# Turning softmax's exponentials by plain products with the identity instead of TensorE's transpose mode

## The chip, the cores and the metric

The kernel runs on one core of one Trainium2 chip. The metric is device time in microseconds (us), median of three runs. The core has TensorE (PE in the profile; its weight loads are PEld), VectorE (DVE), ScalarE (ACT), GpSimd (POOL) and SyncE (SP), each of which works through its own instructions in order and waits on the others by semaphores. Every one of the program's times below is of the whole kernel unless a stretch is named.

## The reference

Eight images of 384 channels and 32 x 32 = 1,024 positions go through two layers, all in fp32. Cut to what matters:

```python
# layer 0: a Mamba block, forward and backward over the 1,024 positions, and a 3x3 depthwise convolution
deltaA  = exp(delta[..., None] * A)                     # 384 channels x 16 states
deltaBu = (delta * u)[..., None] * Bm
h = dA * h + dBu                                        # the scan, step by step
y = einsum('bdn,bn->bd', h, c)                          # summed over the 16 states
...
# layer 1: causal attention with 6 heads of 64, then a feed-forward net with binarized weights
qkv    = x @ Wqkv
scores = einsum('bhqd,bhkd->bhqk', q, k)                # 1,024 x 1,024 for each head
scores = where(causal, scores, -inf)
attn   = softmax(scores, axis=-1)
out    = einsum('bhqk,bhkd->bhqd', attn, v)
out    = out @ Wproj + bproj
...
t = t + attention(layernorm(t)); t = t + feed_forward(layernorm(t))
```

The feed-forward part gives values for five of the eight images (its groups leave the others zero), so the kernel computes it for five.

## The kernel before

The kernel runs the scan of one image beside the attention and feed-forward of the one before it. The steps of both are emitted interleaved, and a scheduler puts each engine's instructions in order. The last image's attention has no scan left to run beside it.

Matrix results go into eight PSUM banks, shared by name; `s` and `pt` have two each:

```python
BANKS = {"y": 1, "da": 2, "s": 2, "pt": 2, "av": 1}
QT = 4              # blocks of 128 queries in a half of 512
...
ptp = ctx.enter_context(tc.tile_pool(name="ptp", bufs=2))
```

The scan works on units of two states. GpSimd multiplies twice for each unit, VectorE scans, and TensorE sums the states into `y`, each block transposed on the way, with the transpose mode. The buffer `g` (7 of them) is free again when that sum has read it.

```python
def s_first(u):
    g = sp.tile([P, 2, HB], F32, name=f"g_{u.name}", tag="g", bufs=7)
    ...
    pin(nc.gpsimd.tensor_tensor(g, ud, sst.pop(("bc", 0, u.name)), ALU.mult))          # L564
...
def s_scan(u):
    ...
        nc.scalar.activation(da, sst["dl", u.b, u.c, u.part], AF.Exp, scale=...)       # L577
        ...
        nc.vector.tensor_tensor_scan(gi[:, ::step], da[:, ::step], gi[:, ::step], ...) # L582
    ...
    pin(nc.gpsimd.tensor_tensor(g, g, sst.pop(("bc", 1, u.name)), ALU.mult))           # L588
...
def s_sum(u):
    ...
    for i in range(2):
        for j in range(QT):
            nc.tensor.matmul(                                                          # L598
                out=y[:, j, :], lhsT=g[:, i, chunk(j)], rhs=ident, is_transpose=True,
                start=(opens and i == 0 and j == 0), stop=(closes and i == 1),
                skip_group_check=True,
            )
```

The attention works on two heads at a time (`e`), over 512 queries (`g`). Scores come with queries on the partitions; the exponentials `pr` leave ScalarE together with their row sums:

```python
def scores(i, qi, n, kb, k0, k1):
    ...
    ss = [bank(f"s_{b}_{c}_{qi}_{kb}_{e}", "s") for e in range(2)]
    for e in range(2):
        nc.tensor.matmul(out=ss[e][:, : k1 - k0], lhsT=st["q"][rows_of(e), c, chunk(qi)],
                         rhs=st["k"][rows_of(e), c, k0:k1], start=True, stop=(k1 < n)) # L753
    ...
    for e in range(2):
        ...
        nc.vector.tensor_reduce(m, s, AX.X, ALU.max, negate=True)                      # L773
        nc.scalar.activation(pr, s, AF.Exp, bias=m, accum_out=rs[:, i, e, kb : kb + 1])# L774
```

To weigh the values, the keys must lie on the partitions. So each 128 x 128 block of `pr` is turned by TensorE into a `pt` bank, ScalarE copies the bank to `ptn`, and the product with `v` sums into `av`. The factors that normalize are spread over the partitions by plain products with the identity:

```python
def spread(kb):
    ...
    nc.tensor.matmul(out=fp[rows_of(e), chunk(i)], lhsT=f.to_broadcast([P, HD]),
                     rhs=ident, start=True, stop=True)                                 # L811
...
def turned(j):
    cols = slice(max(j - g * QT, 0) * P, HB)
    for e in range(2):
        pt = bank(f"pt_{b}_{c}_{g}_{j}_{e}", "pt")
        for i in range(max(j - g * QT, 0), QT):
            nc.tensor.transpose(                                                       # L825
                pt[:, chunk(i)], st["pr", c, g, i, e][:, chunk(j)], ident
            )
        ptn = ptp.tile([P, HB], F32, name=f"ptn_{b}_{c}_{g}_{j}_{e}", tag=f"ptn{e}")
        nc.scalar.copy(ptn[:, cols], pt[:, cols])                                      # L829
        st["ptn", j, e] = ptn

def weigh(j):
    ...
        nc.tensor.matmul(out=av[rows_of(e), cols],
                         lhsT=st["v"][:, j, hd * HD : (hd + 1) * HD],
                         rhs=st["ptn", j, e][:, cols],
                         start=(j % QT == 0), stop=(j % QT == QT - 1))                 # L839
```

For each image and pair of heads, the first 512 queries need 10 turned blocks for a head and the second 512 need 26, as blocks above the diagonal are left out: 36 x 6 heads x 8 images = 1,728 blocks, in 576 banks.

Of the kernel before, what the change touches and what calls it, by code (L numbers as in the profile page):

```python
# [52 lines left out]
def kernel(  # L53
# [16 lines left out]
    nc = tc.nc  # L70
# [11 lines left out]
    def ctile(name, shape, dt=F32):  # L82
        return const.tile(shape, dt, name=name, tag=name)
# [4 lines left out]
    def mtile(name, n=L):  # L88
        return mid.tile([P, n], F32, name=name, tag="mid")
# [7 lines left out]
    def bank(name, tag=None):  # L97
        if tag is None:
            turn[0] += 1
            tag = ("s", "pt")[turn[0] % 2]  # L100
        return ps.tile([P, HB], F32, name=name, tag=tag, bufs=BANKS[tag])

    def half(h):
        return slice(h * HB, (h + 1) * HB)

    def chunk(c):
        return slice(c * P, (c + 1) * P)
# [29 lines left out]
    for d in range(2):  # L137
        nc.scalar.dma_start(out=wdt[d * DW : d * DW + RANK, :], in_=w_dt)
        nc.scalar.dma_start(
            out=wdt[d * DW + RANK : d * DW + RANK + 1, :],  # L140
# [13 lines left out]
    ident = ctile("ident", [P, P])  # L154
# [491 lines left out]
    def attention(b, emit_ffn, emit):  # L646
        st = {}
# [82 lines left out]
        def rows_of(e):  # L730
            return slice(e * HD, (e + 1) * HD)
# [52 lines left out]
        def weighted_values(c, g, steps):  # L784


            last = (g + 1) * QT - 1

            def factors():

                nm, rs = st["nm", c, g], st["rs", c, g]
                st["f", c, g] = mtile(f"f_{b}_{c}_{g}").rearrange("p (k l) -> p k l", k=2)
                if g == 0:
                    nc.vector.reciprocal(rs, rs)
                    return
                low = small.tile([P, QT, 2, 1], F32, name=f"low_{b}_{c}", tag="low")
                nc.vector.tensor_reduce(low, nm, AX.X, ALU.min)
                nc.vector.tensor_tensor(nm, low.to_broadcast([P, QT, 2, 2]), nm, ALU.subtract)
                nc.scalar.activation(nm, nm, AF.Exp)
                nc.vector.tensor_tensor(rs, rs, nm, ALU.mult)  # L800
                nc.vector.tensor_reduce(low, rs, AX.X, ALU.add)
                nc.vector.reciprocal(low, low)
                nc.vector.tensor_tensor(rs, nm, low.to_broadcast([P, QT, 2, 2]), ALU.mult)

            def spread(kb):

                fp = bank(f"f_{b}_{c}_{g}_{kb}")
                for i in range(QT):
                    for e in range(2):
                        f = st["rs", c, g][:, i, e, kb : kb + 1]  # L810
                        nc.tensor.matmul(  # L811
                            out=fp[rows_of(e), chunk(i)],
                            lhsT=f.to_broadcast([P, HD]),
                            rhs=ident,
                            start=True,
                            stop=True,
                        )
                nc.scalar.copy(st["f", c, g][:, kb, :], fp)

            def turned(j):  # L820
                cols = slice(max(j - g * QT, 0) * P, HB)
                for e in range(2):
                    pt = bank(f"pt_{b}_{c}_{g}_{j}_{e}", "pt")
                    for i in range(max(j - g * QT, 0), QT):
                        nc.tensor.transpose(  # L825
                            pt[:, chunk(i)], st["pr", c, g, i, e][:, chunk(j)], ident
                        )
                    ptn = ptp.tile([P, HB], F32, name=f"ptn_{b}_{c}_{g}_{j}_{e}", tag=f"ptn{e}")
                    nc.scalar.copy(ptn[:, cols], pt[:, cols])  # L829
                    st["ptn", j, e] = ptn  # L830

            def weigh(j):
                if j % QT == 0:
                    st["av"] = bank(f"av_{b}_{c}_{g}_{j}", "av")
                av = st["av"]
                cols = slice(max(j - g * QT, 0) * P, HB)
                for e in range(2):
                    hd = 2 * c + e
                    nc.tensor.matmul(  # L839
                        out=av[rows_of(e), cols],  # L840
                        lhsT=st["v"][:, j, hd * HD : (hd + 1) * HD],
                        rhs=st["ptn", j, e][:, cols],
                        start=(j % QT == 0),
                        stop=(j % QT == QT - 1),
                    )
                if j % QT < QT - 1:
                    return
                kb = j // QT
                o, f = st["o"][:, c, half(g)], st["f", c, g][:, kb, :]
                if kb == 0:  # L850
                    nc.vector.tensor_tensor(o, av, f, ALU.mult)  # L851
                else:
                    nc.vector.tensor_tensor(av, av, f, ALU.mult)
                    nc.vector.tensor_tensor(o, o, av, ALU.add)

            for j in range(last + 1):

                @steps
                def _(j=j):
                    if j == 0:  # L860
                        factors()
                    if j % QT == 2:
                        spread(j // QT)
                    turned(j)
                    if j > 0:
                        weigh(j - 1)

            @steps
            def _():
                weigh(last)  # L870
# [302 lines left out]
```

## Time and profile before

| | |
|---|---|
| time, median of 3 runs | 5232.83 us (5232.45 to 5233.16) |
| span of the profiled execution | 5243.0 us |
| granted TensorE clock, mean | 0.864 |
| VectorE busy | 3565.3 us, 68% |
| ScalarE busy | 2726.2 us, 52% |
| turning products (L825): TensorE busy | 312.3 us, 1,728 instructions |
| copies of turned blocks (L829): ScalarE busy | 259.4 us, 576 instructions |
| DMA: moved | 1199.86 MB, mean 229 GB/s |

A line of the profile names a source line of the kernel, an engine, an operation, and what is written and read. "Busy" merges overlapping instructions. TensorE's products overlap one another, and the ends of their records are modelled, so their durations hold a latency; the distance from one start to the next is what a product takes of the engine. In the 40 slices of the page, a digit is a share in tenths of a slice of 131 us. The granted clock is the share of full TensorE clock that was allowed. A wait is idle time of an engine together with the instruction that ended it.

### The profile page before, as it was taken

The numbers are of one execution on the slowest core, as the hardware profiler recorded it, in microseconds if no ns is written. First come the engines' busy times: TensorE is split into PE (matmuls) and PEld (weight loads), VectorE is DVE, ScalarE is ACT, GpSimd is POOL, SyncE is SP. The second block draws the span as 40 slices with busy tenths as digits, with TensorE's granted clock in tenths as the row PEclk, the third lists the DMA queues.
The fourth block names the chain that finished last, engine by engine and source line by source line (L and its number), as shares of the span: only waits on it lengthen the run. The fifth ranks groups of instructions, "written<-read, shape, count | busy, mean of one in ns | idle before, by whom it ended". The sixth has DMA issues, their size and how long they took to land.

```text
span 5243.0 us, 52624 instructions
## 1 busy us (share of the span) xinstructions
PE 4173.2 (80%) x16458; PEld 2200.6 (42%) x16458; DVE 3565.3 (68%) x4249; ACT 2726.2 (52%) x4914; POOL 3674.0 (70%) x1932
## 2 busy tenths in 40 slices
PE   5466566889778889777897788888888888888899
PEld 1223333444334444334443444444444544444444
DVE  6998887667786668766677766677666666566422
ACT  4665554455644555645556445565355354464434
POOL 0477675977768786769876697767787977887700
PEclk7667576989888899889898789998888999999989
DMA  6768678757678567686676875666866866667500
GB/s 227 277 239 283 228 266 284 242 191 263 225 249 292 196 231 240 214 299 227 232 248 223 276 251 201 230 229 231 301 221 211 277 215 239 210 207 236 189 29 25
DMA packets 625121, 1199.86 MB, mean 229 GB/s; under 512 B 44440, under 2 KB 103240, under 8 KB 624840
## 3 DMA queue, kind: packets, MB, share of 16 engines
q1 hardware_dynamic: 615328, 1180.34, 65.6%
q10 hardware_dynamic: 9512, 16.15, 0.9%
q8 instruction: 130, 2.13, 0.2%
q14 instruction: 151, 1.24, 0.1%
HBM read 1030.65 MB, written 165.68 MB: 228 GB/s over the span
## 4 chain that ended last, share of the span: by engine, by line
POOL 32%; issue 20%; PE 13%; DVE 12%; DMA 8%; ACT 4%; SPq 1%; POOLq 0%; DVEq 0%; ACTq 0%
POOL g L564 18%; POOL g L588 13%; DMA bc<-rows 6%; DVE g L582 5%; PE s L753 2%; PE y L598 1%; PE yp L1000 1%; PE qp L697 1%; PE av L839 1%; DVE dp L515 1%; DVE u L362 1%; DVE loc L383 1%; PE hp L955 1%; PE pt L825 1%; PE op L667 1%
## 5 line engine op out<-in xcount | busy, mean ns | idle before, releaser
L564 POOL TENSOR_TENSOR g<-ud,bc 128x1024 f32<-128x1024 f32 x768 | 1830.0, 2383 | 832.9 <-PE y L598 410.4
L588 POOL TENSOR_TENSOR g<-g,bc 128x1024 f32<-128x1024 f32 x768 | 1819.9, 2370 | 311.6 <-issue 135.6
L577 ACT ACTIVATE da<-dl,amat 128x512 f32<-128x512 f32 x1536 | 1057.9, 692 | 1622.5 <-DVE g L582 1577.5
L582 DVE TENSOR_TENSOR_SCAN g<-da,g 128x512 f32<-128x512 f32 x768 | 905.7, 1210 | 551.9 <-POOL g L564 518.2
L598 PE MATMUL y<-ident,g 128*128 128x128 f32 x6144 | 963.2, 304 | 368.3 <-POOL g L588 344.7
L582 DVE TENSOR_TENSOR_SCAN g<-da,carry,g 128x512 f32<-128x512 f32 x768 | 955.4, 1271 | 420.0 <-POOL g L564 399.2
L598 PEld LDWEIGHTS y<-ident,g 128*128 128x128 f32 x6144 | 792.3, 157 | 801.5 <-POOL g L588 480.7
L753 PE MATMUL s<-k,q 64*128 64x512 f32 (+3 forms) x1152 | 464.4, 601 | 177.6 <-ACT pr L774 140.1
L773 DVE TENSOR_REDUCE nm<-s 128x1 f32<-128x512 f32 (+3 forms) x576 | 300.6, 545 | 268.5 <-PE s L762 200.0
L774 ACT ACTIVATE pr<-s,nm 128x512 f32<-128x512 f32 (+3 forms) x576 | 329.5, 575 | 157.5 <-DVE nm L773 150.5
L839 PE MATMUL av<-ptn,v 128*64 128x512 f32 (+3 forms) x1152 | 367.8, 544 | 27.7 <-DVE o L851 22.0
L955 PE MATMUL hp<-t,w 128*128 128x512 f32 x720 | 336.7, 612 | 34.8 <-DMA w<-w1s 20.6
L336 PE MATMUL in<-xn,win 128*128 128x512 f32 x576 | 299.6, 665 | 69.7 <-ACT up L343 36.9
L825 PE MATMUL pt<-ident,pr 128*128 128x128 f32 x1728 | 312.3, 305 | 38.6 <-ACT ptn L829 29.9
L1000 PE MATMUL yp<-h,w 128*128 128x512 f32 x720 | 327.9, 614 | 2.5 <-DMA w<-w2s 2.5
L829 ACT COPY ptn<-pt 128x512 f32<-128x512 f32 (+3 forms) x576 | 259.4, 480 | 125.4 <-PE pt L825 123.6
L753 PEld LDWEIGHTS s<-k,q 64*128 64x128 f32 x1152 | 162.7, 205 | 338.3 <-ACT pr L774 216.9
L825 PEld LDWEIGHTS pt<-ident,pr 128*128 128x128 f32 x1728 | 212.9, 154 | 171.3 <-ACT ptn L829 79.9
L697 PE MATMUL qp<-t,wqk 128*128 128x512 f32 x576 | 265.8, 609 | 13.3 <-DVE t L300 13.3
L383 DVE SCALAR_TENSOR_TENSOR loc<-xn,vec,loc 128x496 f32<-128x496 f32 (+3 forms) x384 | 257.2, 721 | 4.1 <-ACT loc L373 4.0
L362 DVE SCALAR_TENSOR_TENSOR u<-up,vec,u 128x512 f32<-128x512 f32 (+3 forms) x288 | 201.1, 744 | 27.8 <-ACT u L352 27.5
L1000 PEld LDWEIGHTS yp<-h,w 128*128 128x128 f32 x720 | 140.2, 198 | 176.9 <-issue 176.9
(154 smaller groups left out, 4536.6 us busy)
## 6 DMA issues: line engine op xcount, KB each, us to landing
bc<-rows SPq DMA_DIRECT2D x1536, 512.0 KB, 4.9
t<-st SPq DMA_DIRECT2D x63, 512.0 KB, 6.0
su<-u SPq DMA_DIRECT2D x48, 512.0 KB, 4.2
du<-su SPq DMA_DIRECT2D x96, 256.0 KB, 4.7
sdl<-du SPq DMA_DIRECT2D x96, 256.0 KB, 2.9
sud<-du SPq DMA_DIRECT2D x96, 256.0 KB, 3.2
ud<-sud SPq DMA_DIRECT2D x96, 256.0 KB, 5.2
dl<-sdl SPq DMA_DIRECT2D x96, 256.0 KB, 5.6
```

The source lines that it names most:

```text
L564: pin(nc.gpsimd.tensor_tensor(g, ud, sst.pop(("bc", 0, u.name)), ALU.mult))
L577: nc.scalar.activation(da, sst["dl", u.b, u.c, u.part], AF.Exp, scale=amat[:, u.c, n : n + 1])
L582: nc.vector.tensor_tensor_scan(gi[:, ::step], da[:, ::step], gi[:, ::step], first, ALU.mult, ALU.add)
L588: pin(nc.gpsimd.tensor_tensor(g, g, sst.pop(("bc", 1, u.name)), ALU.mult))
L598: nc.tensor.matmul(out=y[:, j, :], lhsT=g[:, i, chunk(j)], rhs=ident, is_transpose=True, start=(opens and i == 0 and j == 0), stop=(closes ...
L697: nc.tensor.matmul(out=qp, lhsT=st["wqk"][:, c, o : o + P], rhs=st["xn"][:, c, half(h)], start=(c == 0), stop=(c == NC - 1),)
L753: nc.tensor.matmul(out=ss[e][:, : k1 - k0], lhsT=st["q"][rows_of(e), c, chunk(qi)], rhs=st["k"][rows_of(e), c, k0:k1], start=True, stop=(k ...
L774: nc.scalar.activation(pr, s, AF.Exp, bias=m, accum_out=rs[:, i, e, kb : kb + 1])
L825: nc.tensor.transpose(pt[:, chunk(i)], st["pr", c, g, i, e][:, chunk(j)], ident)
L839: nc.tensor.matmul(out=av[rows_of(e), cols], lhsT=st["v"][:, j, hd * HD : (hd + 1) * HD], rhs=st["ptn", j, e][:, cols], start=(j % QT == 0 ...
L955: nc.tensor.matmul(out=hp, lhsT=st["w1"][:, c, chunk(m % 2)], rhs=st["xn"][:, c, half(h)], start=(c == 0), stop=(c == NC - 1),)
L1000: nc.tensor.matmul(out=yp, lhsT=st["w2", k // 6][:, k % 6, :], rhs=st["h", k // NC][:, k % NC, half(h)], start=(k == 0), stop=(k == NF - 1),)
```

## The change

The products that turn `pr` lose the transpose mode. The same block is the stationary operand and the same identity the moving one, but the array multiplies and adds in fp32, as in every plain product of this kernel[...]. The result is the same block, turned. Nothing else is edited; the sums of `y`, which use the transpose mode too, stay as they are. The change asks whether the mode is worth having for these blocks.

```diff
--- before.py
+++ after.py
@@ -822,8 +822,12 @@
                 for e in range(2):
                     pt = bank(f"pt_{b}_{c}_{g}_{j}_{e}", "pt")
                     for i in range(max(j - g * QT, 0), QT):
-                        nc.tensor.transpose(
-                            pt[:, chunk(i)], st["pr", c, g, i, e][:, chunk(j)], ident
+                        nc.tensor.matmul(
+                            out=pt[:, chunk(i)],
+                            lhsT=st["pr", c, g, i, e][:, chunk(j)],
+                            rhs=ident,
+                            start=True,
+                            stop=True,
                         )
                     ptn = ptp.tile([P, HB], F32, name=f"ptn_{b}_{c}_{g}_{j}_{e}", tag=f"ptn{e}")
                     nc.scalar.copy(ptn[:, cols], pt[:, cols])
```

The scheduler sees a product of another kind, and so the order of instructions on TensorE, VectorE, ScalarE and the DMA queue differs between the two programs from the first turned blocks on; GpSimd's order is the same.

## Prediction

> **What bounds the kernel now.** I read the page first, for the shape of the whole; then a table of busy time over the stretches in which the softmax runs; then who waits for whom in one of them; last the durations and spacing of TensorE's instructions, for prices. From the page, the busy totals and three rows of its 40 slices (131 us each):
>
> ```profile
> PE 4173.2 (80%) x16458; PEld 2200.6 (42%) x16458; DVE 3565.3 (68%) x4249; ACT 2726.2 (52%) x4914; POOL 3674.0 (70%) x1932
> ...
> PE   5466566889778889777897788888888888888899
> ...
> POOL 0477675977768786769876697767787977887700
> PEclk7667576989888899889898789998888999999989
> ```
>
> From slice 7 on, TensorE (PE) and GpSimd (POOL) are both nearly full; the last two slices belong to TensorE alone. No engine is full throughout, so what counts is what happens where the change is. The turning products (line 825) lie in eight stretches, 216 in each, one per image. The table of busy time by stretch (width, PE, PE weight loads, DVE, ACT, POOL, granted clock, DMA share, GB/s), first and last stretch and the sum of all eight:
>
> ```profile
> 995.00:1218.00 223.00, 186.91 (x988) 100.36 (x986) 144.63 (x179) 128.77 (x300) 181.50 (x94) 0.92 0.62 213
> ...
> 5063.00:5221.00 158.00, 149.46 (x672) 65.58 (x672) 47.58 (x101) 79.58 (x222) 0.00 (x0) 0.89 0.03 11
> sum 1724.00, PE 1463.82 PEld 782.01 DVE 1040.40 ACT 976.07 POOL 1245.19; mean PE 182.98 PEld 97.75 DVE 130.05 ACT 122.01 POOL 155.65
> ```
>
> The last stretch has no scan beside it and TensorE is idle for 158 - 149.5 = 8.5 us of it: TensorE-bound. In the other seven (1,566 us together) PE is busy 1,314 us and idle 252, POOL busy 1,245 and idle 321. Both are 80 to 84% full, and the totals don't say which leads. The waits do. Waits of PE and then of POOL in the stretch 995 to 1218 (us in total, times, longest):
>
> ```profile
> PE s L753 <- ACT pr L774: 17.7, 15, 4.5
> PE f L811 <- DVE rs L803: 5.3, 2, 3.5
> ...
> POOL g L564 <- PE y L598: 36.7, 17, 8.5
> POOL g L564 <- PE s L762: 3.4, 1, 3.4
> ```
>
> POOL is idle 41.5 us there, and 36.7 of it waits for TensorE's y products to free a g buffer. TensorE never waits for POOL there: its own gaps are the softmax's chain (a score bank not yet read by ScalarE). The same two lines lead in the other stretches I opened (46.3 and 46.7 us of POOL's waits at 3114 to 3339 and 4176 to 4409). So in these stretches TensorE, working in order, sets the pace, and POOL follows.
>
> **Prices from the trace.** Durations by line (min/median/max ns): the turning products, and two plain fp32 products for comparison, factors (64 stationary columns) and scores (128):
>
> ```profile
> L825 PEld LDWEIGHTS pt<-ident,pr x1728: 137/141/231, 994.8 to 5221.1; 128*128 128x128 f32 x192
> L825 PE MATMUL pt<-ident,pr x1728: 272/273/477, 994.9 to 5221.2; 128*128 128x128 f32 x192
> ...
> L811 PEld LDWEIGHTS f<-ident,rs x1152: 132/137/232, 1020.1 to 5219.3; 128*64 128x64 f32 x192
> ...
> L753 PEld LDWEIGHTS s<-k,q x1152: 182/186/335, 982.2 to 5199.5; 64*128 64x128 f32 x192
> ```
>
> The code has 1,728 turns, and they are 1,728 instructions. It has 576 factor products, and they are 1,152: a plain fp32 product is two instructions, each with its own weight load. The timeline gives the spacing:
>
> ```profile
> 1999.59 2.56 PE L598 MATMUL y<-ident,g 128*128 128x128 f32 x22
> ...
> 4048.60 5.15 PE ap L896 x12
> ...
> 4601.83 0.55 PE L825 MATMUL pt<-ident,pr 128*128 128x128 f32 x3 [0.91 <-ACT ptn L829]
> ...
> 5132.27 0.49 PE L753 MATMUL s<-k,q 64*128 64x128 f32 x4
> ```
>
> A duration holds a latency that overlaps, so I take spacing. 22 transposes in the y sums: (2.56 - 0.27) / 21 = 109 ns each. Plain: 12 passes of 512 columns in 5.15 us (a piece of the chain) = 429 ns each, so 128 columns take 107 ns a pass. Hence a turn goes from one pass of 109 to two of about 109.
>
> A first product after idleness also shows its weight load. Three transposes took 0.55 us: 0.55 - 0.27 - 0.11 = 0.17 to the second one, 56 over 109. The scores (two heads side by side, two passes) took 0.49: 0.22 to the second pass, some 105 over. So a group that starts cold of weights pays 50 ns more.
>
> **What the Trainium skill says.** "TensorE: Matmul & The Clock Gate", Terms, calls the transpose mode four times faster for FP32. Here both the passes (one against two) and the weight load's visible part (56 against 105 ns) say two. "Perfetto Trace Analysis", Transposes: use transpose rather than a standard matmul; the direction agrees. The first page's Part 4 says that the 8/8 clock doesn't engage for transposes; the trace disagrees, as the 22 above ran at 109 ns, the speed of plain passes. So I count no clock gained merely because the turns become plain. Its LDWEIGHTS section gives columns / 1.2 ns, an estimate of 107 for 128; this agrees with 186 - 137 = 49 ns between 128 and 64 columns and with the 105 above. A plain load thus still fits behind a pass of 109.
>
> **The change in parts.**
> 1. More passes: 1,728 x 109 ns = 188 us at full clock. The stretches have a granted clock near 0.90: 188 / 0.90 = 209 us.
> 2. Weight loads in sight: the turns come in 576 groups (1 to 4 each). I choose half of them as starting bare: 288 x 50 ns = 14 us. In all 223 us of TensorE, 28 for each image.
> 3. Last image: PE is idle 8.5 us of 158, so nearly all counts: 26 us.
> 4. Other seven images: 7 x 28 = 196 us. TensorE is the pace there, but it idles 36 us a stretch, half of that waiting for ScalarE to free a score bank. Work put between two such waits shortens the second; against that, a turned group is delivered up to 0.5 us later (4 x 109 + 50 ns), and the copies to ptn stand in ScalarE's order beside the exponentials. And a fuller TensorE holds its clock longer: 0.90 to 0.93 would give back 3% of 1,314 us, 40 us. I choose half of the 196 as hidden or given back: 98 remain.
> 5. Nothing is moved by hand, but the scheduler orders the program anew. The comparison of the two programs shows POOL's order unchanged and TensorE's equal up to its first turns, then interleaved differently (ScalarE, for instance, takes two pr in a row and then two ptn, where it alternated). I count 0 for it, with some 30 us either way.
>
> Sum: 5233 + 26 + 98 = 5357.
>
> **Rivals.**
> - Hidden: 252 us of idle TensorE would hold 196, and POOL's two lines lead the chain (18% and 13% of the span). Then only the last image pays: about 5259. Against it: POOL's idle time is a wait for this very TensorE.
> - Fully exposed: POOL waits longer for y, and nothing is made up: 5233 + 223 = 5456. For it: TensorE never waits for POOL in the stretches. Against it: the gaps before the scores can close.
> - The clock pays: if the stretches ran at 1.0 in place of 0.90, TensorE's old work would shrink by up to 10% of 1,314 us, and the seven images would cost 196 - 131 = 65, so about 5324. Against it: stretches where TensorE waits for ScalarE keep their pauses.
> - The new order is luckier or worse than the extra work weighs: nothing in the profile of before speaks for a direction.
>
> **Range and chances.** The ends of 8 in 10 lie between "hidden" with a little and "exposed" with a little back: 5285 to 5440. A gain needs an accident of order larger than 100 us on top of a certain cost of 26 us: 2% for faster. Slower by over 2% begins at 5233 x 1.02 = 5338; my centre is 19 us above it, and the longer tail is upward: 62%, with 36% for within 2%.
>
> **What would show it.** The turns are 3,456 instructions with weight loads near 186 ns in place of 141, and spacing near 109 (one of 150 or more would break step 1). TensorE has 18,186 products, and its busy time grows by less than 223 us as spaces fill. POOL stays at 3,674 us busy, but its wait for y grows from about 40 us a stretch to 50 or more, and the seven stretches widen from a mean of 224 us to 238; the last from 158 to 184. The clock in them rises by some hundredths. Up to 995 us nothing changes. I am wrong if the seven keep their width (hidden) or grow by 28 each (exposed), or if the time moves outside of the eight stretches, which would be the new order.

## The result and the profile after

| | before | after |
|---|---|---|
| time, median | 5232.99 us | 5394.94 us |
| ratio, with its 95% interval | | 1.0301 (1.0279 to 1.0323) |
| turning products, instructions | 1,728 | 3,456 |
| span of the profiled execution | 5243.0 us | 5395.1 us |
| seven stretches with scan beside them, sum of widths | 1,566 us | 1,693 us |
| last stretch | 158 us | 170 us |

The kernel became 3.0% slower, 162 us against the 124 that were predicted. The page of the changed kernel, in the lines that answer to those shown of before:

```profile
PE 4316.7 (80%) x18186; PEld 2442.8 (45%) x18186; DVE 3566.0 (66%) x4247; ACT 2739.4 (51%) x4916; POOL 3672.7 (68%) x1932
...
PE   5465566889778889777897788878788888888899
...
POOL 0477676876759676768776687767787877777700
PEclk7667667889879899889898799998899999999999
```

TensorE has 1,728 more products and 143.5 us more of busy time; GpSimd's work is what it was. The picture over the slices looks the same, only longer. By stretch (columns as before: width, PE, weight loads, DVE, ACT, POOL, granted clock, DMA share, GB/s):

```profile
1002.00:1246.00 244.00, 209.53 (x1201) 133.64 (x1200) 144.36 (x178) 131.68 (x303) 179.81 (x93) 0.90 0.60 202
...
5204.00:5374.00 170.00, 163.41 (x895) 96.40 (x895) 47.48 (x101) 81.23 (x224) 0.00 (x0) 0.92 0.03 10
sum 1863.00, PE 1600.63 PEld 1018.90 DVE 1047.85 ACT 996.44 POOL 1247.49; mean PE 200.08 PEld 127.36 DVE 130.98 ACT 124.56 POOL 155.94
```

The eight stretches grew from 1,724 to 1,863 us: 139 of the 152 us by which the two profiles differ. In the seven with scan, TensorE is idle 1,693 - (1,600.6 - 163.4) = 256 us; it was 252. So the extra passes did not fill pauses, by this sum alone. The durations of the turning products (min/median/max ns), and one run of eight passes in the last stretch:

```profile
L825 PEld LDWEIGHTS pt<-ident,pr x3456: 186/192/338, 1001.4 to 5373.5; 128*128 128x128 f32 x192
L825 PE MATMUL pt<-ident,pr x3456: 273/275/583, 1001.5 to 5373.6; 128*128 128x128 f32 x192
```

```profile
5225.00 1.16 PE L825 MATMUL pt<-ident,pr 128*128 128x128 f32 x8
```

Two passes for a turn, and weight loads as long as those of other plain products of 128 columns: as priced. The eight passes fit 6 spacings of 0.11 us, one first of 0.22 (its weight load in sight), and the last duration of 0.27. Waits in the first stretch:

```profile
PE s L753 <- ACT pr L774: 21.2, 16, 3.7
PE pt L825 <- ACT ptn L833: 5.3, 6, 1.1
...
POOL g L564 <- PE y L598: 59.1, 21, 8.3
```

GpSimd waits 59.1 us for the y sums where it waited 36.7. But TensorE's own wait for ScalarE to read a score bank has grown too (17.7 to 21.2). A TensorE with more to do should wait less. And the last stretch grew by 12 us, not 26. These are two things that the price of the passes does not explain. The one part of the change that I had put at zero, the order of instructions, may explain both.

### The profile page after: what moved, and what is told of

Read it like the earlier page. It is cut to its first block, busy times and chain, and to the rows that moved or that the text cites. A ratio compares the mean times of both kernels' runs of the same rounds, so it can differ in the third digit from the quotient of the medians.

```text
span 5395.1 us, 56106 instructions
## 1 busy us (share of the span) xinstructions
PE 4316.7 (80%) x18186; PEld 2442.8 (45%) x18186; DVE 3566.0 (66%) x4247; ACT 2739.4 (51%) x4916; POOL 3672.7 (68%) x1932
## 4 chain that ended last, share of the span: by engine, by line
POOL 30%; issue 22%; DVE 12%; PE 11%; DMA 7%; ACT 4%; SPq 1%; POOLq 0%; DVEq 0%; ACTq 0%
POOL g L564 16%; POOL g L588 14%; DVE g L582 5%; DMA bc<-rows 4%; PE pt L825 2%; PE yp L1004 2%; PE s L753 1%; PE y L598 1%; PE av L843 1%; DVE loc L383 1%; DVE u L362 1%; DVE dp L515 1%; ACT h L984 1%; POOL carry L587 1%; PE qp L697 1%
## 5 line engine op out<-in xcount | busy, mean ns | idle before, releaser
L598 PE MATMUL y<-ident,g 128*128 128x128 f32 x6144 | 952.1, 304 | 375.3 <-POOL g L588 345.3
L582 DVE TENSOR_TENSOR_SCAN g<-da,carry,g 128x512 f32<-128x512 f32 x768 | 955.4, 1270 | 429.4 <-POOL g L564 408.9
L753 PE MATMUL s<-k,q 64*128 64x512 f32 (+3 forms) x1152 | 430.3, 588 | 198.6 <-ACT pr L774 161.8
L825 PE MATMUL pt<-ident,pr 128*128 128x128 f32 x3456 | 541.7, 306 | 41.3 <-ACT ptn L833 34.4
L825 PEld LDWEIGHTS pt<-ident,pr 128*128 128x128 f32 x3456 | 477.1, 214 | 145.7 <-ACT ptn L833 65.1
L843 PE MATMUL av<-ptn,v 128*64 128x512 f32 (+3 forms) x1152 | 306.3, 536 | 9.9 <-DVE o L855 9.9
L959 PEld LDWEIGHTS hp<-t,w 128*128 128x128 f32 x720 | 134.8, 196 | 191.7 <-issue 154.6
```

The lines of the kernel that those rows point to most:

```text
L598: nc.tensor.matmul(out=y[:, j, :], lhsT=g[:, i, chunk(j)], rhs=ident, is_transpose=True, start=(opens and i == 0 and j == 0), stop=(closes ...
L825: nc.tensor.matmul(out=pt[:, chunk(i)], lhsT=st["pr", c, g, i, e][:, chunk(j)], rhs=ident, start=True, stop=True,)
L843: nc.tensor.matmul(out=av[rows_of(e), cols], lhsT=st["v"][:, j, hd * HD : (hd + 1) * HD], rhs=st["ptn", j, e][:, cols], start=(j % QT == 0 ...
L959: nc.tensor.matmul(out=hp, lhsT=st["w1"][:, c, chunk(m % 2)], rhs=st["xn"][:, c, half(h)], start=(c == 0), stop=(c == NC - 1),)
```

## Experiments: the order apart from the passes

The scheduler fixes every engine's order when the program is built. So a kernel can be planned with one kind of turning product and then run with the other: the mode is changed when all orders stand. In both kernels below, nothing but the mode differs from the program whose order they have. The edit, shortened:

```diff
     with tile.TileContext(nc) as tc:
         tile_conv_attn_hybrid_kernel(tc, *args)
+    for block in nc.main_func.blocks:
+        for k, ins in enumerate(block.instructions):
+            if turns_pr(ins):                        # the 1,728 turning products
+                block.instructions[k] = copy.replace(ins, is_transpose=mode)
```

**Order of the changed program, transpose mode.** Theories: A, the new order gave something back (heads side by side more often); B, it is neutral; C, it does harm.

> The order of instructions of the changed program on every engine, but the turning products in transpose mode again (1,728 single passes). Theory A, the price is larger than what was measured and the new order gave a part back: the profile after shows turning products up by 229 us of TensorE over the eight stretches, and av down by 55 and scores down by 32, because heads stand side by side more often (single av products 105 in place of 205); then this kernel is faster than before, near 5190 us (5160 to 5215). Theory B, the order is neutral and about a third of the price was hidden in TensorE's pauses: 5233 within 10. Theory C, the new order does harm and the price is small: 5260 or more.

Measured: 5351.76 us, ratio 1.0224 (1.0193 to 1.0254). Each ratio from here on is to the kernel before, timed again beside the run (medians of 5,236 to 5,246 us).

**Order of before, plain turns.**

> The order of instructions of the program before on every engine, but the turning products plain (3,456 passes). Theory A: nearly the whole price shows, 5435 us (5410 to 5460). Theory B: as the changed kernel, 5395 within 10. Theory C: 5370 or less.

Measured: 5311.64 us, ratio 1.0147 (1.0118 to 1.0175). Together with before and after:

| ratio to before | transpose mode | plain |
|---|---|---|
| order of before | 1 | 1.0147 |
| order of the changed program | 1.0224 | 1.0301 |

C holds in both. The passes cost 1.5% in the old order, 77 us; in the new order the step from 1.0224 to 1.0301 is 0.8%. The order alone costs 2.2% with transposes and 1.5% with plain turns. A and B fall: av products and scores did become cheaper in the new order, as theory A says, but the new order is slower all the same. The third stretch and the sum over the seven, from the table of busy time of before, of the new order with transposes, and of the old order with plain turns:

```profile
2414.00:2631.00 217.00, 182.88 (x992) 100.31 (x990) 143.90 (x178) 127.86 (x300) 179.70 (x93) 0.92 0.64 224
...
sum 1566.00, PE 1314.36 PEld 716.43 DVE 992.82 ACT 896.49 POOL 1245.19; mean PE 187.77 PEld 102.35 DVE 141.83 ACT 128.07 POOL 177.88
```

```profile
2455.00:2699.00 244.00, 188.66 (x997) 107.26 (x996) 145.08 (x180) 131.10 (x304) 181.97 (x95) 0.86 0.61 203
...
sum 1688.00, PE 1322.10 PEld 743.60 DVE 1010.74 ACT 910.57 POOL 1252.81; mean PE 188.87 PEld 106.23 DVE 144.39 ACT 130.08 POOL 178.97
```

```profile
2435.00:2664.00 229.00, 201.91 (x1205) 127.35 (x1204) 148.24 (x179) 128.47 (x298) 179.77 (x95) 0.95 0.62 212
...
sum 1616.00, PE 1443.11 PEld 899.22 DVE 995.34 ACT 904.89 POOL 1245.49; mean PE 206.16 PEld 128.46 DVE 142.19 ACT 129.27 POOL 177.93
```

Read width less PE as TensorE's pauses. Old order, plain: PE is busy 129 us more and idle 79 less (252 to 173), so 50 us remain. New order, transposes: PE is busy only 8 us more and idle 114 more (252 to 366): the order's loss is pauses. And after: from 366 the plain turns then took 110 away (to 256), at 115 more of busy time, which leaves 5 us. So most of the passes' time was hidden in pauses, and the pauses were new. The equality of 252 and 256 had hidden both.

The granted clock moved as well. Its mean over the seven stretches is 0.897 before, 0.863 in the new order with transposes, 0.936 in the old order with plain turns and 0.907 after. So PE's 8 us are two things: at the clock of before, its 1,322 us would be some 1,270 (an estimate, 1,322 x 0.863 / 0.897), so the new order made TensorE's work cheaper by some 45 us and the lower clock took that back. And the clock took up a part of the plain turns too: the step from 0.863 to 0.907 is worth some 64 us of 1,322, the step from 0.897 to 0.936 some 55 us of 1,314 (estimates). Why the clock was lower in the new order is not shown.

What the new pauses are, in the third stretch. Before (PE, ACT, DVE, POOL):

```profile
PE s L753 <- ACT pr L774: 17.1, 16, 2.7
...
ACT da L577 <- DVE g L582: 60.6, 45, 5.0
...
DVE g L582 <- POOL g L564: 53.1, 27, 9.2
...
POOL g L564 <- PE y L598: 36.0, 13, 9.0
```

The new order with transposes:

```profile
PE s L753 <- ACT pr L774: 30.7, 17, 5.9
PE pt L825 <- ACT ptn L833: 7.2, 4, 2.6
...
ACT da L577 <- DVE g L582: 74.7, 55, 6.0
...
DVE g L582 <- POOL g L564: 73.9, 29, 8.2
...
POOL g L564 <- PE y L598: 57.3, 17, 8.1
```

TensorE waits longer for ScalarE to read its score and turn banks; ScalarE stands longer at da, the scan's exponentials, which wait for VectorE; that one waits for GpSimd, and GpSimd for TensorE's y sums to free a g buffer. This is a ring, in which each engine has in its queue, behind what it waits for, what the next one needs. Over the seven stretches, the waits of TensorE for pr before a score went from 122 to 176 us, and for ptn before a turn from 27 to 75: 102 of the 114 us of new pauses. (In the order of before, the plain turns shortened the first of these waits, to 97 us.)

**Only the last image plain**, in the order of before; there is no scan and no such ring.

> The order of the program before, with only the last image's 216 turning products plain; no scan runs beside them. The prediction's step 3 said that nearly all of 26 us counts there; the profile after shows the last stretch longer by 11 only. If the step is right and the new order gave the rest back (theory A): 5255 to 5260. If the stretch hides half by itself (theory B): 5244 within 3.

Measured: 5257.16 us, ratio 1.0044 (1.0026 to 1.0062), 23 us. Its last stretch is 185 us wide, with PE busy 180, against 158 and 149.5. Nearly nothing is hidden where TensorE has hardly any pauses. In the changed kernel the stretch grew by 12 only since the new order shortens it: 149 us with transposes, PE busy 136.5. The last stretch of this run, and that of the new order with transposes:

```profile
5046.00:5231.00 185.00, 180.36 (x891) 100.28 (x889) 47.32 (x101) 81.35 (x223) 0.00 (x0) 0.89 0.03 9
...
5176.00:5325.00 149.00, 136.50 (x681) 63.35 (x682) 47.63 (x101) 79.25 (x224) 0.00 (x0) 0.93 0.03 11
```

This run also shows how far a width can be trusted. Its seven stretches hold the same work in the same order as before, and are 1,543 us wide in its profile for 1,566: 23 us between two profiles of the same work. The new order's 122 us stand well clear of that. The 50 us of the plain turns are borne out by the time: 77 us less this run's 23.

In the new order the two heads of a pair stand side by side more often, and that is worth something to TensorE. In the whole program, 205 av products stand alone (with no product of the other head beside them) in the order of before and 105 in the new one. What it is worth can be seen in the timeline of before, one head's two passes and both heads' four:

```profile
5136.69 0.86 PE L839 MATMUL av<-ptn,v 128*64 128x384 f32 x2
...
5169.12 0.87 PE L839 MATMUL av<-ptn,v 128*64 128x384 f32 x4
```

**One head of each pair plain**, in the order of before: half of the passes.

> The order of the program before, with the turning products of one head of each pair plain (864 of 1,728). If TensorE's pauses swallow a first part of the extra work (the prediction's step 4, and theory B), the first half costs less than half of all: under 60 us over before. If TensorE sets the pace all along (theory A), half of the price of the full change in this order, about 100 us: 5320 to 5345.

Measured: 5256.17 us, ratio 1.0054 (1.0038 to 1.0069), 28 us (20 to 36), of which the last stretch (169 us wide for 158) has some 11. The seven stretches:

```profile
sum 1565.00, PE 1358.89 PEld 800.84 DVE 993.15 ACT 896.21 POOL 1245.62; mean PE 194.13 PEld 114.41 DVE 141.88 ACT 128.03 POOL 177.95
```

PE is busy 45 us more and the width is as before, within those 23 us. TensorE's pauses fall by 46 us (252 to 206), and the clock's mean rises from 0.90 to 0.93, worth some 50 us of 1,314 (an estimate). The second half adds 84 us of busy time and 51 of width; the pauses fall by another 33, and the clock rises by less than 0.01 more. By the times, this half of the passes costs 28 us, where half of 77 would be 38. That is somewhat less than in proportion; that the first half is free is not shown. It agrees with step 4 in its kind, and theory A's rate falls.

## Experiments: what in the order costs

I counted, in the two programs, how many units ahead of the y sums the scan's da stand when a pr or ptn follows them on ScalarE, taking TensorE's place from the score or turn that it belongs to. It is 7.2 (pr) and 6.9 (ptn) before, 7.35 and 7.3 in the new order, with seven g buffers. Theory L says that this nearness to the limit closes the ring.

**Another plan, the same work:** the y sums planned as plain products, then set back to the transpose mode, as above; turns in transpose mode throughout.

> All turns and all y sums in transpose mode, as before; but the scheduler planned with the y sums as plain products, so the order differs and the work does not. Theory L (lead): the two orders so far differ in how far ScalarE's exponentials for the scan (da) stand ahead of TensorE's y sums when a softmax copy or exponential follows them: 6.9 units ahead of ptn and 7.2 ahead of pr before, 7.3 and 7.35 after the change, with seven g buffers as the limit; the nearer the limit, the more ScalarE stands at a da that can't run while TensorE waits for the pr or ptn behind it. Here the lead is 7.2 and 7.5, so the time should be like that of the changed order with transposes: 5310 to 5380. Theory P (pairs): av and score products of two heads side by side decide; here pairs are more (av singles 116, scores 99 against 205 and 231), so it should be faster than before: under 5220.

Measured: 5334.35 us, ratio 1.0177 (1.0147 to 1.0207). As theory L says, and against P: with more heads side by side than before it is slower. Half of its loss is in the seven stretches (1,610 us), the rest elsewhere, and for that half theory L gives no reason.

**A neighbouring plan.**

```diff
-JOINT = 0.6
+JOINT = 0.62
```

> One planning constant (JOINT) 0.62 in place of 0.60: another order, the same work, the lead as before (6.95 and 7.2 units). Theory L: within 20 us of before. Rival R (the order before had been chosen by trial among many, and any other loses): slower by 40 us or more.

Measured: 5268.66 us, ratio 1.0057 (1.0035 to 1.0079), 22 to 30 us over before. That is a little over theory L's limit of 20, and below R's 40. Its seven stretches are 1,549 us wide, no more than before, so what it lost lies outside of them. The order of before does lose a little when one constant moves; but by a quarter of what the new order lost.

**The y sums first** (shortened; the precedence is set once around both loops):

```diff
         for i in range(2):
             for j in range(QT):
-                nc.tensor.matmul(
+                with tc.high_priority(offset=200): nc.tensor.matmul(
                     out=y[:, j, :],
```

> The y sums get precedence in TensorE's planning (offset 200), turns in transpose mode; the lead falls to 5.5 (ptn) and 6.0 (pr) units, and heads stand apart more often. Theory L: faster than before, 5120 to 5200, with ScalarE's wait at da falling under 350 us in the seven stretches (397 before, 489 in the changed order with transposes). Theory P or R: slower than before.

Measured: 5208.41 us, ratio 0.9943 (0.9923 to 0.9962). Faster than before, if not by as much as expected. The third stretch:

```profile
PE s L754 <- ACT pr L775: 10.0, 12, 1.8
...
ACT da L577 <- DVE g L582: 37.7, 37, 3.7
...
DVE g L582 <- POOL g L564: 36.0, 25, 6.6
...
POOL g L564 <- PE y L599: 11.5, 8, 3.3
```

All four waits of the ring are shorter at once, though the heads stand apart more often (269 single av products for 205). Over the seven stretches ScalarE's wait at da is 287 us, under the 350 that were expected (397 before), and TensorE's pauses are 167:

```profile
sum 1530.00, PE 1363.13 PEld 738.16 DVE 1035.42 ACT 919.05 POOL 1322.60; mean PE 194.73 PEld 105.45 DVE 147.92 ACT 131.29 POOL 188.94
```

The stretches do not hold quite the same work as before: GpSimd is busy 1,323 us in them for 1,245, as more of the scan falls into them.

**Heads together.** The first head's product also waits for what the second's waits for, and the second (of the av products, both) gets precedence. Shortened:

```diff
+                    with tc.high_priority(offset=60):
+                        made = nc.tensor.matmul(out=av[rows_of(e), cols], ...)
+                    if e == 0:
+                        together(made, st["copied", j, 1])   # waits for the copy of the other head, too
+                    else:
+                        pin(made)
                     # the same for the scores, with the exponentials that free the other bank
```

> The first head's av and score products also wait for what the second head's wait for, so that both run side by side (av singles 3 in place of 205, scores 52 in place of 231); the lead is 6.1 and 6.4 units. Theories L and P both say faster: 5090 to 5190, with av at about 30 us of TensorE a stretch in place of 40. Rival R: slower. If it is slower with av and scores cheaper, waiting for the second head costs more than its separate pass.

Measured: 5248.64 us, ratio 1.0005 (0.9994 to 1.0016): no difference. The seven stretches:

```profile
sum 1637.00, PE 1239.22 PEld 733.48 DVE 1083.18 ACT 937.43 POOL 1369.22; mean PE 177.03 PEld 104.78 DVE 154.74 ACT 133.92 POOL 195.60
```

PE's busy time in them fell to 1,239 us from 1,314, and its pauses rose to 398 from 252. The stretches became wider and took in more of the scan (POOL 1,369 us for 1,245), and the rest of the kernel became shorter. So L and P were both wrong about the time, and so was R: by the total, waiting for the second head costs about what its separate pass costs.

**The changed program with the y sums first.** The edit of the y sums above, in the changed kernel.

> The changed program (turns plain, planned as plain) with precedence for the y sums (offset 200): the lead falls from 7.3 (ptn and pr) to 6.7 units. Theory L: the loss of the order goes, the price of the second passes stays: 1.005 to 1.015 of before (5265 to 5320). If the order's loss in the changed program has another cause than late y sums: 1.025 or more.

Measured: 5460.69 us, ratio 1.0426 (1.0405 to 1.0447). Slower than the changed kernel, against theory L's number. Here the plan is made with the dearer turns again; PE's pauses in the seven stretches are 222 us, fewer than the 256 after, but ScalarE's wait at da is 517 us where it was 466 after, though the count of units ahead is smaller. Other things differ as well: 214 av products stand alone for 105, PE is busy 1,573 us in them (after: 1,437), and more of the scan lies in the same stretches (POOL 1,400 us for 1,247).

**Plain turns in the order with y first**, by the change of mode after planning.

> The order of the kernel with y first (5208 us, 0.9943 of before), with the turning products plain. In the order of before the plain turns cost 76 us, because TensorE's waits fell by 77 us in the seven stretches and the clock rose. With y first TensorE waits 165 us there in place of 249, so there is less to swallow. If pauses are what hides the passes: 100 to 150 us over y first, 1.013 to 1.023 of before. If the same 76 shows: about 1.009.

Measured: 5287.85 us, ratio 1.0098 (1.0079 to 1.0117). From 0.9943 that is 1.56%, some 81 us, and in the order of before it was 77: the second of the two expectations. Even with fewer pauses to begin with, the plain turns found some: in the seven stretches PE is busy 1,481 us of 1,587, so the pauses fell from 167 to 106, and the clock's mean in these stretches rose from 0.92 to 0.97.

**More precedence for y: offset 1000, and 400.**

> The y sums go as soon as they can in the plan (offset 1000), turns in transpose mode; lead 4.7 (ptn) and 5.1 (pr) units. Theory L alone: faster than y first at 200 (under 5208, 0.994). If the softmax, held up by the y sums, then sets the end: slower than that, with longer stretches.

> The same with offset 400, lead 5.1 (ptn) and 5.5 (pr): between the two, 0.988 to 0.998 of before; the best order of these if the gain has its optimum between 200 and 1000.

Measured: 5586.16 us, ratio 1.0671 (1.0647 to 1.0694), and 5526.89 us, ratio 1.0556 (1.0536 to 1.0575). Both are much slower, so theory L alone doesn't hold. The third stretch at offset 1000:

```profile
PE y L599 <- POOL g L588: 31.9, 18, 3.8
...
POOL g L564 <- PE y L599: 59.9, 3, 25.6
```

Now TensorE stands at y sums whose g isn't there yet (176 us over the seven stretches; none before), with the softmax behind them, and GpSimd waits for y three times, but once for 25.6 us. The ring closes from the other side. The stretches account for 182 of the 333 us by which this profile is longer than that of before (1,748 us for 1,566); the rest lies outside of them and was not followed up.

So it is shown that the order alone, with the same work, moves this kernel between 0.994 and 1.067, and that the new order's loss is pauses of TensorE in the seven stretches, nearly all in waits for ScalarE. By the estimate above, a lower clock took back what its cheaper work saved. That y sums come late against the scan's front is supported by three runs (the new order, y first, and the y plan for half of its loss), is not contradicted by the neighbour, and is refuted as the only cause by three (y first in the changed program, and the two higher offsets). Which feature of the new order makes most of its 2.2% stays open. An order of one engine from one program and of another from the other was not tried.

## Why the prediction was right, and where it was not

The time lay in the range, and the direction held. By its own steps:

1. **Passes and their price: right.** 3,456 instructions, weight loads of 192 ns for the 186 named, a median spacing of 112 ns between neighbouring passes at full clock for 109. The busy time of line 825 rose from 312.3 to 541.7 us by the page, 229 us for the 223 of steps 1 and 2.
2. **Weight loads in sight:** a choice of 14 us that no run separates from the passes.
3. **Last image, 26 us: right as a price** (23 us, interval 14 to 32, in the order of before), **but it didn't appear whole** in the changed kernel (12 us), for the order gave back some 9 us there.
4. **Half of 196 us hidden or given back: right in kind, off in size.** In the order of before 50 us remained of it, so three quarters were taken up: by 79 us of pauses and by a clock that rose from 0.90 to 0.94 (means over the seven stretches), as that step named both. In the order of the changed kernel 5 us remained. The clock rose with the plain turns in all three orders: 0.90 to 0.94, 0.86 to 0.91, and 0.92 to 0.97 with the y sums first.
5. **"I count 0 for it, with some 30 us either way": the step that failed.** The new order costs 117 us with transposes, 83 with plain turns (5394.94 - 5311.64), four times and three times what I allowed. With transposes it adds 114 us of pauses to TensorE, in the ring of waits shown above.

The sum came out near by luck, because the errors were of opposite sign: 98 expected in step 4 against some 50, and 0 in step 5 against some 83. For the passes, the order of before lies midway between the rival "hidden" (26 us) and my centre (124) with its 77 us, and the new order nearer to "hidden" with 43. The rival of the order was the larger half of the result. I had dismissed it with "nothing in the profile of before speaks for a direction". That was so; but a tuned kernel's order is something it can lose, and that I could have weighed.

What was named as signs: GpSimd's busy time stayed (3,672.7 us), its wait for y passed 50 us a stretch (59.1 in the first), and the seven widened to a mean of 242 us (238 named). The clock rose by 0.01 where some hundredths were named, and the last stretch reached 170 us, not 184. The mark for "wrong" that I set, growth outside of the stretches as the sign of a new order, was a bad mark: the order did its harm inside of them, and only the same work in two orders tells the two apart.

## What to carry to other kernels

Where a scheduler plans the program, an edit of one instruction's kind is two changes: its price, and a new plan. Separate them by planning with the one kind and running the other, before any of the difference is put down to the instruction. Pauses that are the same before and after may be different pauses: compare who waits for whom. And for turning fp32 blocks, take the transpose mode: it is one pass where a plain product is two.

The kernel with the y sums first (offset 200, turns in transpose mode) beats both, 5208.41 us and 0.9943 of before.

## What the runs showed that I had not expected

- Order alone, with identical work on every engine, spans 0.994 to 1.067. A precedence of 200 gains 0.6% and of 400 loses 5.6%.
- Half of the extra passes, 864 of them, cost 28 us where all cost 77. The seven stretches, in which TensorE is 84% busy, are as wide with them as before (1,565 us for 1,566) and 51 us wider with the other half, though two profiles of the same work differ by 23 us there.
- Two heads' av products, each on 64 of the array's columns, take as long as one head's alone: four passes in 0.87 us, two in 0.86. Yet an order that forces the heads together gains nothing, as TensorE's busy time only becomes waiting.
